# Turning the neighbour sums of a graph layer once, with the repeats made by transfers in SBUF, and one-hots made two sets ahead

## The chip, the cores and the metric

The kernel runs on one core of one Trainium2 chip. The metric is device time in microseconds (us). The engines are called as in the profile: PE is TensorE's matmul (PEld its weight load), DVE is VectorE, ACT is ScalarE, POOL is GpSimd, and SP is SyncE, which here only issues DMAs.

## What is computed

Two graph layers on 6250 nodes with 160 features (64 scalars and 32 vectors of three components) and 100000 edges sorted by target. The first layer, whose last part the change is in, sums messages by node and then takes a tensor product of each node's own features with its sums:

```python
msgs = _merge(m0 + d0, m1 + d1)
agg = jax.ops.segment_sum(msgs, row, num_segments=N)
a0, a1 = _split(agg)                       # 64 scalars, 32 x 3
x0, x1 = _split(node_features)
u0, u1 = _tp(x0, x1, a0, a1, wu000, wu011, wu101, wu110)
ud0, ud1 = _lin(x0, x1, lu0, lu1)
return node_features + _merge(u0 + ud0, u1 + ud1)
# in _tp:
out0 = (einsum('eu,ev,uvw->ew', x0, y0, w000) + INV_SQRT3 * einsum('euk,evk,uvw->ew', x1, y1, w110)) / sqrt(fan0)
out1 = (einsum('eu,evk,uvw->ewk', x0, y1, w011) + einsum('euk,ev,uvw->ewk', x1, y0, w101)) / sqrt(fan1)
```

The second layer gathers, gates and sums again. Here it is enough that it follows.

## The kernel before

Three stages follow each other. `scatter` makes the messages of the edges and writes each to the place in DRAM that its node's bin (25 nodes) has; `update` does the rest of the first layer; `windows` is the second layer. Only `update` is touched.

`update` works by groups of 500 nodes: twelve full ones and one of 250. Features lie on partitions and nodes along the row. For one group:

- `fetch` (L683) loads messages into `urec`, four bins (a set) at a time, 322 KB a bin, by SP's queue. It is called after the set that frees the buffer has been summed; there are three buffers. A group has five sets.
- `sums` (L696) is a generator, with a yield where other work may come between. For each set, `ones` (L702) makes one-hots of the messages' nodes: ACT computes `rl`, then 16 squares (L719) and one Relu (L722) into `uhot`; for group 0 DVE does it instead. PE then sums the set by 16 matmuls (L734), ACT copies the sums into `ag` (L740, L742), and the one-hots of the next set are made.
- After the last set the sums are turned, so that features come to lie on partitions: matmuls of `ag` with `quad` (L755), copied by ACT into `a` (L751). `a` is 128 x 4 x 500. The product needs the 64 scalar sums twice and each 32 vector sums four times over the 128 partitions, so `ag` holds its columns already repeated, and the turning is done four times, once for each part of `a`.
- `Group.first` makes products. A step of kind y, x or v multiplies weights or features on PE into PSUM (L833, L852; two buffers), and DVE multiplies the result with `a` or with `x1k` (L837, L855). POOL adds products of y and v (L840, L860) and prepares parts of v with `a` in `ahead` (L822), from `xb`, which `repeat` (L815) loads. `second` (L868) sums products on PE.
- `back` (L875) finishes a group during the next one: it adds the result to the node's features (L898), normalises (L909 to L920, into `uh`), turns again (L930, `uT` L933), multiplies with the next layer's weights (L940, L941) and stores rows of the table T1 from `utt` (L945, L946; two buffers).

The order on PE, DVE, ACT and POOL is written out by hand: the loop at the end of `update` goes through 32 steps of a group in the pattern y, x, v, x, and in each calls `next` some times on the next group's `sums` and on the last group's `back`:

```python
for _ in range((2, 2, 0, 1)[r % 4] if r >= 3 and g + 1 < len(groups) else 0):
    next(gs[g + 1].sums, end)
for _ in range((1, 2, 0, 1)[r % 4]):
    while backs and next(backs[0], end) is end:
        backs.pop(0)
```

So where a matmul of `sums` falls depends on how many yields stand before it. The order of DMAs on SP's queue is not written out; a scheduler sets it when the kernel is built. SP takes its queue in order, and each DMA there waits for its inputs, for its buffer, and, as the eight semaphores of these DMAs are used in turn, for the DMA that had its semaphore before.

The sums of group 0 have no earlier group to run beside; they are made ahead of the loop.

Of the kernel before, what the change touches and what calls it, by code (L numbers as in the profile page):

```python
# [13 lines left out]
F32 = mybir.dt.float32  # L14
# [9 lines left out]
P = 128  # L24
M0, M1 = 64, 32
V = 3 * M1
F = M0 + V
# [6 lines left out]
BW = 25  # L34
# [22 lines left out]
def gnn_kernel(ctx: ExitStack, tc: tile.TileContext, a: dict, out: bass.AP):  # L57
    nc = tc.nc
# [564 lines left out]
    def update():  # L623
# [3 lines left out]
        with ExitStack() as s:  # L627
            wp = s.enter_context(tc.tile_pool(name="uw", bufs=1))
            pool = s.enter_context(tc.tile_pool(name="u", bufs=1))
            two = s.enter_context(tc.tile_pool(name="u2", bufs=2))  # L630
# [7 lines left out]
            pt = s.enter_context(tc.tile_pool(name="pt", bufs=2, space=PSUM))  # L638
# [33 lines left out]
            quad = wp.tile([P, 4, BW], F32, name="quad")  # L672
# [10 lines left out]
            def fetch(k):  # L683

                if k >= len(quads):
                    return
                g, q = quads[k]
                b0, nq = groups[g][0] // BW + q, min(4, groups[g][1] // BW - q)
                got[g, q] = recs.tile([P, 4, 4, F + 1], F32, name="urec")
                for b in range(nq):  # L690
                    with tc.issue_after(last[-1]) if last else nullcontext():
                        at = nc.sync.value_load(start_i[0:1, b0 + b:b0 + b + 1], min_val=0, max_val=E)
                    last.append(nc.sync.dma_start(got[g, q][:, b], msgs[bass.ds(at, CAP), :]
                                                  .rearrange("(p i) f -> p i f", i=4)).ins)

            def sums(g, a):  # L696

                r0, n = groups[g]
                qs = [(q, min(4, n // BW - q)) for q in range(0, n // BW, 4)]
                hots, ags = [], []  # L700

                def ones(q, nq):  # L702


                    rl = two.tile([P, 4, 4], F32, name="rl")
                    nc.scalar.activation(rl[:, :nq], got[g, q][:, :nq, :, F], AF.Copy, scale=-1.0,
                                         bias=float(r0 + q * BW))
                    hot = two.tile([P, 4, 4, 32], F32, name="uhot")
                    hots.append(hot)
                    if g == 0:  # L710
                        nc.vector.tensor_tensor(hot[:, :nq].rearrange("p b i n -> p i b n"),
                                                node[:, None, :nq].to_broadcast([P, 4, nq, 32]),
                                                rl[:, :nq].rearrange("p b i -> p i b")[:, :, :, None]
                                                .to_broadcast([P, 4, nq, 32]), op=OP.add)
                        nc.vector.tensor_single_scalar(hot[:, :nq], hot[:, :nq], 0.0, op=OP.is_equal)
                        return
                    for b in range(nq):
                        for i in range(4):
                            nc.scalar.activation(hot[:, b, i], node[:, b], AF.Square, bias=rl[:, b, i:i + 1])  # L719
                        if b % 2:  # L720
                            yield
                    nc.scalar.activation(hot[:, :nq], hot[:, :nq], AF.Relu, scale=-1.0, bias=1.0)  # L722
                    yield

                yield from ones(*qs[0])
                yield
                for j, (q, nq) in enumerate(qs):
                    if g == 0 and j + 1 < len(qs):
                        yield from ones(*qs[j + 1])
                    p = pt.tile([P, 4 * P], F32, name="ptr")  # L730
                    rec, hot = got.pop((g, q)), hots.pop(0)
                    for i in range(4):
                        for b in range(nq):
                            nc.tensor.matmul(p[32 * b:32 * b + 32, :F], hot[:, b, i], rec[:, b, i, 0:F],  # L734
                                             start=i == 0, stop=i == 3, tile_position=(0, 32 * b))
                    fetch(quads.index((g, q)) + 3)
                    yield
                    w = 32 * nq
                    ag = pool.tile([P, 4, P], F32, name="ag", bufs=5)
                    nc.scalar.copy(ag[:w, 0].rearrange("p (i f) -> p i f", i=2),  # L740
                                   p[:w, None, 0:M0].to_broadcast([w, 2, M0]))
                    nc.scalar.copy(ag[:w, 1:].rearrange("p k (i f) -> p k i f", i=4),  # L742
                                   p[:w, M0:F].rearrange("p (k f) -> p k f", k=3)[:, :, None]
                                   .to_broadcast([w, 3, 4, M1]))
                    ags.append(ag)
                    if g and j + 1 < len(qs):
                        yield from ones(*qs[j + 1])
                    yield
                for j in range(5):
                    if j:  # L750
                        nc.scalar.copy(a[:, j - 1, :n], p[:, :n])  # L751
                    if j < 4:
                        p = pt.tile([P, 4 * P], F32, name="ptr")
                        for ag, (q, nq) in zip(ags, qs):
                            nc.tensor.matmul(p[:, q * BW:(q + nq) * BW], ag[:32 * nq, j],  # L755
                                             quad[:32 * nq, :nq].rearrange("p b n -> p (b n)"), start=True, stop=True)
                        yield

            def loads(g, n):

# [27 lines left out]
            class Group:  # L788
                def __init__(self, g):
                    self.g = g  # L790
                    self.r0, self.n = groups[g]
                    self.a = two.tile([P, 4, 4 * P], F32, name="a")
                    self.side = loads(g, self.n)
                    self.sums = sums(g, self.a)
                    self.early = {}
                    self.begun = False
# [981 lines left out]
```

## Time and profile before

| | us |
|---|---|
| median of 3 runs (lowest to highest) | 3754.78 (3748.99 to 3765.18) |
| the profiled execution | 3762.7 |
| its span | 3760.6 |
| scatter, in the span | 0 to 1376 |
| sums of group 0 | 1376 to 1411 |
| update of all groups | 1411 to about 2337 |
| windows | about 2337 to 3760 |

The profile shows one execution. A group of its lines stands for all instructions of one line of code on one engine. A wait is written as who waited, on what, for whom, with the total of us, the number and the longest. In a timeline a line has its start, its length, the engine, the line of code, the operation, out<-in and a count, and in brackets the idle time before it and what ended it.

### The profile page before, as it was taken

Reading aid. Unit: us, or ns where it says so; the run is one execution under the profiler, and the core shown is the slowest. Engines: PE = TensorE matmul, PEld = TensorE weight load, DVE = VectorE, ACT = ScalarE, POOL = GpSimd, SP = SyncE. Lnnn points to the kernel's source line nnn. Section 1 sums busy time; section 2 is a strip of 40 time slices with the busy share of each in tenths; the row PEclk is TensorE's granted clock in tenths of the full one; section 3 lists DMA queues with packets and bytes.
Section 4 is the critical chain, followed back from the end, with each engine's and each line's share of the span. In section 5 each row is a group of like instructions: output and inputs, shape, how many; then the busy total and the mean of one; then the engine's idle time right before and its main releaser. Section 6 shows DMA issues by size and latency. Waiting matters only on the chain. (4 is left out here: it accounts for less than half of the span.)

```text
span 3760.6 us, 47934 instructions
## 1 busy us (share of the span) xinstructions
PE 2411.6 (64%) x12112; PEld 1273.7 (34%) x12112; DVE 2218.5 (59%) x4577; ACT 1547.0 (41%) x5126; POOL 2219.3 (59%) x1864
## 2 busy tenths in 40 slices
PE   5555565565544439999999998455655565655655
PEld 3433343343333323333333333132323333332323
DVE  7665555555444427777777775455555556555554
ACT  4554444554444424544453441333434333433433
POOL 4655555555666537777777775655555555555552
PEclk8677767776666659999999999566666666666666
DMA  6655555555444456665565532445444454445442
GB/s 176 172 162 162 151 160 174 153 171 153 135 132 130 135 178 179 181 181 159 173 182 176 165 116 70 130 131 147 133 136 132 135 141 139 132 134 146 134 132 71
DMA packets 346121, 554.56 MB, mean 147 GB/s; under 512 B 63954, under 2 KB 245168, under 8 KB 339947
## 3 DMA queue, kind: packets, MB, share of 16 engines
q1 hardware_dynamic: 229160, 288.49, 27.7%
q0 software_dynamic: 87584, 218.31, 19.9%
q10 hardware_dynamic: 29091, 44.61, 3.6%
q8 instruction: 99, 1.62, 0.2%
q14 instruction: 187, 1.53, 0.1%
HBM read 418.16 MB, written 133.04 MB: 147 GB/s over the span
## 5 line engine op out<-in xcount | busy, mean ns | idle before, releaser
L563 POOL DMA_INDIRECT msgs<-rec,pos_i x782 | 782.5, 1001 | 568.2 <-issue 223.9
L1060 POOL DMA_INDIRECT wgot<-T,src_i x782 | 741.3, 948 | 636.0 <-issue 423.7
L543 PE MATMUL rank<-seen,every 128*128 128x256 f16 x782 | 261.2, 334 | 449.3 <-ACT junk L556 296.5
L556 ACT ACTIVATE junk<-rank,off 128x256 bf16<-128x256 f32 x782 | 373.2, 477 | 403.5 <-remote 284.5
L545 PE MATMUL pmsg<-tw,d 120*128 120x160 f32 x1564 | 463.4, 387 | 79.8 <-issue 68.8
L1079 PE MATMUL wgate<-wrad,wblk 97*128 97x480 f32 x522 | 378.6, 858 | 175.0 <-issue 133.3
L855 DVE TENSOR_TENSOR pr<-y,a 128x1000 f32<-128x1000 f32 (+1 forms) x312 | 352.7, 1153 | 132.7 <-PE y L852 131.9
L840 POOL TENSOR_TENSOR pr<-pr 128x1500 f32<-128x1500 f32 (+1 forms) x104 | 338.1, 3251 | 149.1 <-DVE pr L837 149.1
L1097 DVE TENSOR_TENSOR whot<-lane,wbank 128x192 f32<-128x192 f32 x131 | 45.9, 350 | 619.4 <-ACT wbank L1205 550.1
L1216 PE MATMUL wbank<-wms,whot 128*32 128x160 f32 x1564 | 255.7, 411 | 213.6 <-ACT wo L1220 104.5
L545 PEld LDWEIGHTS pmsg<-tw,d 120*128 120x128 f32 x1564 | 317.0, 251 | 147.4 <-issue 93.4
L1091 ACT ACTIVATE wm<-wgot,wattr 128x160 f32<-128x160 f32 x782 | 311.1, 398 | 34.9 <-DMA wgot<-T,src_i 12.6
L560 DVE CAST pos_i<-pos 128x4 int32<-128x4 f32 x196 | 42.4, 216 | 419.1 <-ACT junk L556 347.5
L1216 PEld LDWEIGHTS wbank<-wms,whot 128*32 128x32 f32 x1564 | 146.4, 144 | 405.9 <-ACT wo L1220 137.5
L1094 ACT ACTIVATE wsg<-wgate 128x480 f32<-128x480 f32 x259 | 137.5, 566 | 352.7 <-remote 187.7
L860 POOL TENSOR_TENSOR ppr<-ppr,pr 128x1000 f32<-128x1000 f32 (+1 forms) x104 | 232.0, 2231 | 79.5 <-DVE pr L855 77.1
L544 PEld LDWEIGHTS <-upto 128*128 128x128 bf16 x782 | 91.6, 117 | 541.5 <-issue 499.3
L544 PE MATMUL rank<-hot,upto 128*128 128x256 bf16 x782 | 262.2, 335 | 0.5 <-DVE hot L528 0.5
L531 DVE TENSOR_TENSOR seen<-seen,hot 128x256 f16<-128x256 f16 x782 | 230.5, 295 | 45.5 <-DVE hot L528 7.6
L528 DVE TENSOR_SCALAR hot<-binb,qb 128x256 bf16<-128x256 bf16 x782 | 242.7, 310 | 0.0
L1079 PEld LDWEIGHTS wgate<-wrad,wblk 97*128 97x128 f32 x522 | 131.2, 285 | 314.2 <-issue 239.6
L1115 DVE TENSOR_TENSOR wm<-wm,wtb 128x384 f32<-128x384 f32 (+1 forms) x393 | 221.8, 564 | 13.5
(215 smaller groups left out, 4430.2 us busy)
## 6 DMA issues: line engine op xcount, KB each, us to landing
urec<-msgs SPq DMA_DIRECT2D x250, 322.0 KB
attb<-in_attr SPq DMA_DIRECT2D x48, 960.0 KB
tw<-T0s SPq DMA_DIRECT2D x391, 75.0 KB
xb<-hT SPq DMA_DIRECT2D x192, 125.0 KB
dstb<-in_dstrow SPq DMA_DIRECT2D x48, 480.0 KB
T0s<-tt ACTq DMA_DIRECT2D x11, 1200.0 KB
msgs<-rec,pos_i POOLq DMA_INDIRECT x782
wgot<-T,src_i POOLq DMA_INDIRECT x782
```

What stands on the lines that cost most here:

```text
L528: nc.vector.tensor_scalar(hot, binb, qb[:, t:t + 1], None, op0=OP.is_equal)
L543: nc.tensor.matmul(rank[:, j % 2], every, before, start=True, stop=False)
L544: nc.tensor.matmul(rank[:, j % 2], upto, hot, start=False, stop=True)
L545: nc.tensor.matmul(prs[-1][:, j % 2, :F], ds[j // WP][:, j % WP], tws[j // WP], start=True, stop=True)
L556: nc.scalar.activation(junk, rank, AF.Relu, bias=off, accum_out=pos[:, j:j + 1])
L563: nc.gpsimd.indirect_dma_start(out=views[(t0 + j) % NV][:, :], out_offset=bass.IndirectOffsetOnAxis(ap=pos_i[:, j:j + 1], axis=0), in_=rec ...
L840: nc.gpsimd.tensor_tensor(prs[0], prs[0], prs[1], op=OP.add)
L855: nc.vector.tensor_tensor(pr[:, :, :n], y[:, :, :n], a[:, j, None, :n].to_broadcast([P, 2, n]), op=OP.mult)
L1060: nc.gpsimd.indirect_dma_start(out=got[u][:, i], out_offset=None, in_=T1[:, :], in_offset=bass.IndirectOffsetOnAxis(ap=src_i[:, t0 + i:t0 ...
L1079: nc.tensor.matmul(p[:, :n], blocks[u // CH][:, u % CH], rad[:, lo * F:lo * F + n], start=True, stop=True)
L1091: nc.scalar.activation(m[:, b, j:j + F], g[:, i, oS1:oS1 + F], AF.Copy, scale=attr(u)[:, i, 0:1])
L1216: nc.tensor.matmul(state["acc"][j:j + WN], hot[:, i], ms[:, i], start=t0 + i == w * WT, stop=t0 + i == end, tile_position=(0, j))
```

## The change

`ag` becomes a plain copy of a set's 160 sums. The turning is done twice: columns 0 to 127 (the 64 scalars and the first two vector components) and columns 128 to 159. ACT copies each of the four parts once into `a`, at the partitions where it comes out of the matmul, and DMAs within `a` fill the other partitions: one of 64 rows and nine of 32 rows of 2000 bytes a group. They go by SP's queue; for group 0 six of the ten go by ACT's. The one-hots of two sets are made before the first set is summed (except in group 0), and those of set j + 2 after set j; `rl` and `uhot` get a third buffer. The number of yields in `sums` changes with it.

```diff
@@ -702,10 +702,10 @@
                 def ones(q, nq):
 
 
-                    rl = two.tile([P, 4, 4], F32, name="rl")
+                    rl = two.tile([P, 4, 4], F32, name="rl", bufs=3)
                     nc.scalar.activation(rl[:, :nq], got[g, q][:, :nq, :, F], AF.Copy, scale=-1.0,
                                          bias=float(r0 + q * BW))
-                    hot = two.tile([P, 4, 4, 32], F32, name="uhot")
+                    hot = two.tile([P, 4, 4, 32], F32, name="uhot", bufs=3)
                     hots.append(hot)
                     if g == 0:
                         nc.vector.tensor_tensor(hot[:, :nq].rearrange("p b i n -> p i b n"),
@@ -722,7 +722,8 @@
                     nc.scalar.activation(hot[:, :nq], hot[:, :nq], AF.Relu, scale=-1.0, bias=1.0)
                     yield
 
-                yield from ones(*qs[0])
+                for q, nq in qs[:1 if g == 0 else 2]:
+                    yield from ones(q, nq)
                 yield
                 for j, (q, nq) in enumerate(qs):
                     if g == 0 and j + 1 < len(qs):
@@ -736,25 +737,26 @@
                     fetch(quads.index((g, q)) + 3)
                     yield
                     w = 32 * nq
-                    ag = pool.tile([P, 4, P], F32, name="ag", bufs=5)
-                    nc.scalar.copy(ag[:w, 0].rearrange("p (i f) -> p i f", i=2),
-                                   p[:w, None, 0:M0].to_broadcast([w, 2, M0]))
-                    nc.scalar.copy(ag[:w, 1:].rearrange("p k (i f) -> p k i f", i=4),
-                                   p[:w, M0:F].rearrange("p (k f) -> p k f", k=3)[:, :, None]
-                                   .to_broadcast([w, 3, 4, M1]))
+                    ag = pool.tile([P, F], F32, name="ag", bufs=5)
+                    nc.scalar.copy(ag[:w], p[:w, 0:F])
                     ags.append(ag)
-                    if g and j + 1 < len(qs):
-                        yield from ones(*qs[j + 1])
+                    if g and j + 2 < len(qs):
+                        yield from ones(*qs[j + 2])
                     yield
-                for j in range(5):
-                    if j:
-                        nc.scalar.copy(a[:, j - 1, :n], p[:, :n])
-                    if j < 4:
-                        p = pt.tile([P, 4 * P], F32, name="ptr")
-                        for ag, (q, nq) in zip(ags, qs):
-                            nc.tensor.matmul(p[:, q * BW:(q + nq) * BW], ag[:32 * nq, j],
-                                             quad[:32 * nq, :nq].rearrange("p b n -> p (b n)"), start=True, stop=True)
-                        yield
+
+
+                for lo, hi in ((0, P), (P, F)):
+                    p = pt.tile([P, 4 * P], F32, name="ptr")
+                    for ag, (q, nq) in zip(ags, qs):
+                        nc.tensor.matmul(p[:hi - lo, q * BW:(q + nq) * BW], ag[:32 * nq, lo:hi],
+                                         quad[:32 * nq, :nq].rearrange("p b n -> p (b n)"), start=True, stop=True)
+                    yield
+                    for j, at, w in ((0, 0, M0), (1, M0, M1), (2, M0 + M1, M1)) if lo == 0 else ((3, 0, M1),):
+                        nc.scalar.copy(a[at:at + w, j, :n], p[at:at + w, :n])
+                        for to in range(0, P, w):
+                            if to != at:
+                                (nc.scalar if g == 0 and to // w % 2 else nc.sync).dma_start(
+                                    a[to:to + w, j, :n], a[at:at + w, j, :n])
 
             def loads(g, n):
 
```

## The prediction

> **What bounds the kernel now.** I read the 40 slices first, then the busy time by stage, then who waits for whom inside the stage that the change touches, then one group of that stage in order of time.
>
> ```profile
> PE   5555565565544439999999998455655565655655
> ...
> PEclk8677767776666659999999999566666666666666
> ```
> ```profile
> 1376.00:1411.00 35.00, 18.10 (x200) 14.09 (x200) 5.60 (x10) 5.66 (x18) 0.00 (x0) 0.53 0.90 269
> 1411.00:2256.00 845.00, 783.36 (x5125) 290.80 (x5123) 650.38 (x606) 379.82 (x1392) 628.86 (x232) 0.99 0.57 168
> ```
>
> The first fence has the slices: those with 9s on PE are the update (1411 to 2330 us), the only stage in the diff. The second has two stages (length, then busy us of PE, PEld, DVE, ACT, POOL, then PE's clock, DMA share, GB/s). In the update PE is busy 783 of 845 us, at a clock of 0.99; DVE, POOL and ACT have 23%, 26% and 55% to spare. So work taken off PE is worth its time, unless another wait grows. The 35 us before it, when group 0 is summed, are DMA-bound (share 0.90), with PE half idle. A group of 500 nodes takes 73.2 us and has 32 steps, in fours y, x, v, x; I number them 0 to 31.
>
> ```profile
> L755 PEld LDWEIGHTS ptr<-quad,ag x504: 183/192/338, 1404.6 to 2255.8; 128*128 128x128 f32 x168
> L755 PE MATMUL ptr<-quad,ag x504: 272/275/537, 1404.6 to 2255.9; 128*128 128x100 f32 x168
> ```
> ```profile
> PE ptr L734 <- ACT uhot L722: 17.6, 10, 1.9
> PE y L852 <- DVE pr L837: 12.8, 20, 1.1
> PE ptr L734 <- DVE uxo L898: 9.7, 9, 1.1
> PE ptr L940 <- ACT utt L945: 6.1, 10, 0.6
> PE ptr L894 <- ACT ag L742: 3.1, 10, 0.3
> PE ptr L755 <- ACT utt L945: 2.4, 2, 1.6
> ```
>
> The first two lines are the turning, by the tile ag; the others are PE's own waits over ten steady groups (us in total, times, longest). The wait for one-hots, L734 on L722, is the largest: 1.76 us a group.
>
> ```profile
> 1907.25 2.73 PE L755 MATMUL ptr<-quad,ag 128*128 128x100 f32 x20
> 1909.82 0.59 PE L852 MATMUL y<-x,pick 96*128 96x500 bf16 x2
> 1910.33 1.06 PE L868 MATMUL out<-pr,w_f 128*64 128x500 f32 x4
> 1911.32 2.48 PE L755 MATMUL ptr<-quad,ag 128*128 128x100 f32 x20
> 1913.63 0.59 PE L852 MATMUL y<-v,pickv 96*128 96x500 bf16 x2
> ```
> ```profile
> 1899.66 4.15 SPq L693 DMA_DIRECT2D urec<-msgs  x4
> 1903.91 0.85 SPq L946 DMA_DIRECT2D T<-utt  x2
> 1904.85 0.97 SPq L815 DMA_DIRECT2D xb<-hT  x2
> 1908.59 0.29 SPq L946 DMA_DIRECT2D T<-utt  x1
> 1908.93 1.71 SPq L815 DMA_DIRECT2D xb<-hT  x4
> ```
> ```profile
> 1908.09 0.48 ACT L945 COPY utt<-ptr 116x384 f32<-116x384 f32 x1 [6.27 <-DMA T<-utt]
> ```
>
> This is the tail of one group in order of time, on PE, SP's queue and ACT (start, us, instruction). Twenty turning matmuls hold PE 2.31 us (1911.32 to 1913.63), 0.1155 us each. In the middle ACT stands 6.27 us on a store of T1 that SP could only issue after the four loads of urec; PE's second turning needs the PSUM buffer which that ACT copy empties.
>
> **The change part by part.** *Turning.* The 504 instructions become 252. Group 0 loses 20; groups 1 to 11 lose 20 each and the half group 6 of 12: 11 x 20 + 12 = 232 in the PE-bound stage, 232 x 0.1155 = 26.8 us saved. The second turning has 32 stationary columns; I give it the same pitch, since 100 columns stream either way. If it were as short as L734's with 32 columns (0.04 us an instruction), up to 9 us more would go.
>
> *ACT.* The two copies into ag (266 and 484 ns) become one of 160 columns; between those rows that is about 0.29 us, so 0.46 us less, five times a group. The copies into a stay four; fewer partitions do not shorten them (L751, 576 ns for 500 columns). ACT has room, so both count as nothing while that holds.
>
> *Ten transfers a group within a* (one of 128 KB, nine of 64 KB). No such row exists. Issue: the nearest is xb on the same queue, four in 1.71 us, so ten take 4.3 us. Landing: in group 0 POOL starts on xb 3.3 us after the last of its loads is issued (1414.3 to 1417.65); urec of 322 KB, four issued from 1389.27, is used at 1396.17. A rule of the Trainium skill speaks against this part: DMA: Bandwidth & Descriptors, section "Anatomy of one DMA", gives (for the GpSimd path) about 2.0 us fixed plus bytes at 436 GB/s, and its "Bandwidth" section calls transfers under 64 KB dominated by descriptors. By it, taken one after another, ten cost 10 x 2.15 = 21.5 us; by the rows above they overlap, 4.3 + 3.3 = 7.6 us. I take the rows. From the start of the second turning: ACT's last copy ends 2 us later, SP issues from 0.6 to 5, the last lands at about 8. The next group's first y, where PE (L833), DVE (L837) and POOL (L822) all need a, comes after 12.3 us (1908.62 to 1923.25 in the trace of this group, less the 2.3 removed). So the repeats are hidden with some 4 us to spare; behind them on SP stands x0 of a later group, which waits for PE's last y anyway. Their 0.7 MB add a twentieth to a group's traffic (173 GB/s over 73 us).
>
> *One-hots two sets ahead.* In the built order, the sums' matmuls (L734) move from steps 5, 9, 13, 17, 21 to 8, 12, 16, 20, 21. The 1.76 us wait goes. What is late next? SP's order moves too: two loads of xb now precede the fetch of the fourth set, and they wait until POOL has read the old xb (L822, 1793.26 to 1795.57 in the group that starts at 1774.41). The fetch starts near 1796.4, needs 3.8 us to issue and 2 to 3 to land: 1802.4 to 1803.3. ACT's one-hots of that set now stand ahead of the normalisation of the group before. From there ACT needs 3.7 + 1.1 + 1.9 (uh) + 0.6 + 0.3 + 3.7 (the fifth set) + 1.0 (uT) = 12.3 us, so uT is ready at 1814.7 to 1815.6. PE reaches the matmul on uT (L940) at about 1814.5; from there to the fifth set's matmul it has 6.8 us, now with the fourth set's in between: 1821.5 to 1822.4, against 1822.36 in the trace. So the wait that goes comes back almost whole as waits for uh, uT and DVE: gain 0 to 0.8 us a group. I take 0.3, 3 us in all; bounds are the whole 17.6 us and, by one more such ACT delay, -10.
>
> *The T1 store.* Fourth and fifth sets are now fetched back to back: 8 x 322 KB in 8 us, issued at 339 GB/s, while DMA here reaches 268 to 287 GB/s. The backlog grows from about 0.5 to 1.2 us; the T1 store behind it lands 0.7 us later, then ACT's utt copy, then PE's second turning, which now has no slack (2.4 us of waits in ten groups): -0.7 x 10 = -7 us, bounds 0 and -15.
>
> *Group 0.* Nothing hides its repeats. SP is issuing urec until 1411.36, so its four transfers go out at 1411.4 to 1413.1 and land about 1416; six go by ACT's queue, some 0.4 us each between the copies. DVE started at 1412.40: -3.5 us, bounds -1 and -6.
>
> The third buffers of rl and uhot are paid for by the smaller ag and cost nothing. Scatter and windows stages keep their instructions.
>
> Sum: 26.8 + 3 - 7 - 3.5 = 19 us off the profiled execution's 3762.7 (span 3760.6 plus 2.1 around it). That execution lies 0.2% above the median shown, 3754.78; the same share gives 3736. A measurement of this kernel can tell about 0.5%, 18.8 us, from no change, so the likeliest case ends almost on that bound.
>
> **The rivals.** *A: one-hots ahead pay in full.* If urec lands early and uh is not late, all 17.6 us go and the T1 store costs 2: 26.8 + 17.6 - 2 - 3.5 = 39 us, 3716. For it: the wait was named in every group. Against it: the SP order and the ACT chain above. *B: the waits eat it.* DVE paces steps 4 to 12 (PE loses the filler of one sums matmul there, DVE has uxo and statistics to add) and the bad bounds of one-hots and T1 store hold: 26.8 - 10 - 15 - 3.5 = -2 us, 3757, no change. For it: PE already waits on L837 and L898. *C, slower: the repeats land late.* Its place is the first y of each group. It takes over from a last landing 12.3 us after the second turning starts, and each us beyond costs 11; from 14 us on the gain is gone. Taken one by one at 2.15 us, the last lands at 22.1, 9.8 late: 108 - 19 = 89 us slower, 3844; with a third of that lateness, 3772. For it: the SP queue is in order and waits for ACT there. Against it: four xb loads issue in 1.7 us without waiting for each other. That the change fails to take work off PE can be excluded: the built order has half the turnings.
>
> **How the numbers follow.** Likeliest case 0.42 (3728 to 3746, half of it past 0.5%), A 0.26, B 0.19 (a little of it slower), C 0.13. Faster by over 0.5%: 0.21 + 0.26 + a little of B's good end = 0.49. Slower: C and B's bad end, 0.14. Within: 0.37. The range goes from A with shorter second turnings, 3706, to the mild end of C, 3774.
>
> **What would show it.** L755 (now L751) has 252 instructions; PE busy in 1411 to 2256 falls by about 27 us. PE's wait of L734 for uhot is gone; in its place PE waits for uT before the first L940 and for utt before the second turning, 0.5 to 1 us each. DVE's first multiply of a group never waits for a transfer within a, except in group 0, where it starts 3 to 4 us later. A group takes 71.5 to 72 us. Wrong: a group under 70.5 us (A); DVE or PE waiting on a's transfers at every group's first step (C); PE busy down by 27 us but groups still at 73 us (B).

## The result and the profile after

The changed kernel takes 3767.43 us (median), the kernel before 3756.39 us beside it: ratio 1.0026, 95% interval 1.0016 to 1.0036, some 10 us slower, inside the 0.5% that was set as the bound. The prediction had it 19 us faster. A second measurement (e8 below) gave 1.0011 (0.9996 to 1.0027). So the change costs a few microseconds, where 19 were forecast as won.

The kernels below were measured in several rounds, not all on one chip: the kernel before took 3756, 3078, 3726, 3762 and 3077 us in them. Each ratio is to the kernel before in the same round. What differs between the rounds lies outside the update; the loop over groups inside it, from the first to the last product of x with the self weights (L804 before), does not move with it, so I compare *loops* across runs: 872.2 us before (869.9 in e11) and 870.8 after (861.0 in e8, and 869.3 in e3, whose loop has the same code, in the round at 3078). One execution of a loop is good to some 5 us either way.

First the slices of the page of the changed kernel, then its stage of 845 us that answers to 1411:2256 (length, busy us of PE, PEld, DVE, ACT, POOL, PE's clock, DMA share, GB/s), and the turning by its tile:

```profile
PE   5555555656444438889899898356655555555655
...
PEclk8666677767666658999999999566666666666666
```
```profile
1424.50:2269.50 845.00, 762.88 (x4890) 266.50 (x4891) 649.68 (x606) 353.66 (x1314) 627.44 (x232) 0.97 0.61 176
```
```profile
L751 PE MATMUL ptr<-quad,ag x252: 204/275/536, 1410.5 to 2266.6; 128*128 128x100 f32 x62, 128*32 128x100 f32 x62, 64*128 64x50 f32 x1, 64*32 64x50 f32 x1
```

The turning has half its instructions and PE is busy 20 us less in the stage. But the digits of PE in the update went from 9 to 8 and 9, and its clock from 0.99 to 0.97: the work went away and time did not. Who PE waits for in ten steady groups (us, times, longest):

```profile
PE y L854 <- DVE pr L839: 16.6, 30, 1.1
PE ptr L751 <- ACT utt L947: 11.0, 9, 3.5
PE y L835 <- DVE pr L857: 10.8, 18, 0.7
PE ptr L896 <- DVE uxo L900: 8.7, 5, 4.3
PE ptr L942 <- ACT uT L935: 6.5, 10, 1.6
PE ptr L942 <- ACT utt L947: 6.1, 10, 0.6
PE y L854 <- DVE pr L857: 5.1, 10, 0.5
```

The wait for one-hots is gone, as forecast, and most others have grown or are new: 69 us in all against 54 before. The line to follow is `uxo`. DVE adds the finished group to uxo, and waits for its load; first the changed kernel, then the kernel before, from the waits of DVE in the same ten groups:

```profile
DVE uxo L900 <- DMA uxo<-xs: 19.2, 9, 5.5
```
```profile
DVE uxo L898 <- DMA uxo<-xs: 4.1, 2, 3.9
```

The tail of the group that starts at 1799.18, on SP's queue and on ACT, answers to the tail shown before:

```profile
1840.12 8.29 SPq L693 DMA_DIRECT2D urec<-msgs  x8
1848.52 1.66 SPq L948 DMA_DIRECT2D T<-utt  x2
...
1853.79 0.29 SPq L948 DMA_DIRECT2D T<-utt  x1
1854.25 6.98 SPq L758 DMA_DIRECT2D a<-a  x10
```
```profile
1853.29 0.48 ACT L947 COPY utt<-ptr 116x384 f32<-116x384 f32 x1 [7.67 <-DMA T<-utt]
```

Eight fetches stand back to back, and the T1 store behind them keeps ACT 7.67 us in place of 6.27. Behind the store come the ten transfers, 6.98 us on SP's queue.

Group 0, on SP and on DVE, and DVE's first product before:

```profile
1394.89 26.24 SPq L693 DMA_DIRECT2D urec<-msgs  x20
1421.24 2.53 SPq L758 DMA_DIRECT2D a<-a  x4
```
```profile
1426.24 1.72 DVE L839 TENSOR_TENSOR pr<-y,a 128x1500 f32<-128x1500 f32 x1 [18.18 <-DMA a<-a]
```
```profile
1412.40 1.72 DVE L837 TENSOR_TENSOR pr<-y,a 128x1500 f32<-128x1500 f32 x1 [10.31 <-PE y L833]
```

DVE's first product starts 13.84 us later than before. Of these, 6.3 us are another end of scatter in that execution: ACT's first `rl` is at 1384.06 against 1377.74, and in e9 and e10, where nothing of group 0 is by transfers, the loop's start (1423.4 and 1426.9 against 1416.8 before) wanders as far. From that `rl` to DVE's first product it is 42.18 us after and 34.66 before: 7.5 us are the change's.

### The profile page after: what moved, and what is told of

Same layout as the page of the kernel before. It is cut to its first block, busy times and chain, and to the rows that moved or that the text cites. A ratio compares the mean times of both kernels' runs of the same rounds, so it can differ in the third digit from the quotient of the medians.

```text
span 3766.4 us, 47528 instructions
## 1 busy us (share of the span) xinstructions
PE 2388.1 (63%) x11860; PEld 1249.2 (33%) x11860; DVE 2213.0 (59%) x4577; ACT 1521.9 (40%) x5063; POOL 2214.9 (59%) x1864
## 5 line engine op out<-in xcount | busy, mean ns | idle before, releaser
L545 PE MATMUL pmsg<-tw,d 120*128 120x160 f32 x1564 | 471.6, 393 | 69.5 <-issue 58.4
L1081 PE MATMUL wgate<-wrad,wblk 97*128 97x480 f32 x522 | 368.9, 839 | 161.3 <-issue 122.2
L839 DVE TENSOR_TENSOR pr<-y,a 128x1500 f32<-128x1500 f32 (+1 forms) x104 | 172.2, 1656 | 101.4 <-PE y L835 75.5
```

The costliest lines, as they stand in the source:

```text
L545: nc.tensor.matmul(prs[-1][:, j % 2, :F], ds[j // WP][:, j % WP], tws[j // WP], start=True, stop=True)
L1081: nc.tensor.matmul(p[:, :n], blocks[u // CH][:, u % CH], rad[:, lo * F:lo * F + n], start=True, stop=True)
```

## The experiments

Three questions: what does the halved turning bring by itself, what do its transfers cost and by what, and what do the one-hots cost? Theory 1 after reading the trace was that the transfers cost only in group 0 and that the one-hots' new order on SP makes uxo late; theory 2 that the transfers make it late.

**e1: turning and transfers alone.** The kernel before, with these lines of the change and nothing of the one-hots:

```diff
+                    ag = pool.tile([P, F], F32, name="ag", bufs=5)
+                    nc.scalar.copy(ag[:w], p[:w, 0:F])
...
+                for lo, hi in ((0, P), (P, F)):
```

> The turning and its ten transfers of the changed kernel; the one-hots as before (one set ahead, two buffers). Theory 1 (the one-hots two ahead cost more than they save, by the order on SP: uxo and T1 stores later; the transfers cost only in group 0): PE loses its 27 us, no new waits in the steady groups, group 0 costs about 7 us: 20 us under the kernel before, ratio 0.995 (0.993 to 0.996). DVE's wait for uxo stays near 4 us in ten groups. Theory 2 (the transfers themselves load SP's queue and the DMA engines in each group and make the other loads late): no faster than before, 0.998 to 1.003, with the uxo wait near 19 us here too.

Measured: ratio 0.9993 (0.9982 to 1.0003), loop 859.8 us, DVE's wait for uxo 32.4 us in ten groups. Theory 1 fails: uxo is late without any change of the one-hots. SP's queue at a group's end and the next one's begin shows why; behind it are the loads of x1 and uxo of the kernel before, in the group of the prediction:

```profile
1419.85 6.25 SPq L755 DMA_DIRECT2D a<-a  x10
1426.14 1.07 SPq L814 DMA_DIRECT2D xb<-hT  x2
1427.31 0.48 SPq L761 DMA_DIRECT2D x<-hT  x1
1428.15 1.25 SPq L766 DMA_DIRECT2D x1k<-hT  x3
1438.57 0.31 SPq L763 DMA_DIRECT2D x<-hT  x1
...
1442.73 1.80 SPq L814 DMA_DIRECT2D xb<-hT  x4
1444.58 0.86 SPq L307 DMA_DIRECT2D uxo<-xs  x2
```
```profile
1781.68 0.32 SPq L764 DMA_DIRECT2D x<-hT  x1
...
1784.59 0.85 SPq L307 DMA_DIRECT2D uxo<-xs  x2
```

At 1429.4 the queue stops for 9 us: L763 loads x1, whose one buffer is free only when PE has multiplied the old x1 (L804 there). Behind that stop are eleven loads that stand ahead of uxo, among them four of xb; uxo goes out 6.0 us after x1. Before, five loads stood between the two and uxo followed 2.9 us after x1. With ten transfers ahead of the stop, six loads that stood there before have come behind it: four of xb, one of x1k and one of x3. In the changed kernel three of xb stand there (issued from 1876.00, after the tail above).

The lateness costs twice. PE's clock in stretches around one such wait (same columns as above), and two of its instructions:

```profile
1370.90:1374.30 3.40, 1.74 (x9) 0.56 (x7) 0.88 (x2) 3.11 (x13) 1.65 (x1) 1.00 0.80 216
1374.30:1374.90 0.60, 0.02 (x1) 0.00 (x0) 0.60 (x2) 0.00 (x0) 0.00 (x0) 0.52 0.91 176
1374.90:1381.10 6.20, 6.20 (x17) 1.74 (x19) 5.39 (x6) 0.00 (x0) 5.25 (x3) 0.50 0.67 207
```
```profile
1373.80 0.43 PE L893 MATMUL ptr<-both,u 128*128 128x64 f32 x2 [1.66 <-DVE uxo L897]
...
1374.90 1.20 PE L832 MATMUL y<-x,w_f 64*128 64x500 f32 x1 [0.58 <-DVE pr L854]
```

PE waits 1.66 us and works 0.5; then, as a second wait of 0.58 us only begins, the granted clock is half, and it stays so for over 6 us: the same matmul that took 0.68 us takes 1.20. The Trainium skill ("TensorE: Matmul & The Clock Gate", "HAM oscillation — how this bites in real kernels") has the rule that gaps of PE beyond about 3.4 us bring the half clock; here it came after one of 1.66 us. Such a wait does not always bring it: PE waits up to 1.9 us for one-hots in every group of the kernel before, at a clock of 0.99. What decides it is not shown here.

**e6: the turning without transfers**, as e1, with a set to zero once and no DMA within it, so that the repeats are left out:

```diff
-                    self.a = two.tile([P, 4, 4 * P], F32, name="a")
+                    self.a = abuf[g % 2]
...
-                        for to in range(0, P, w):
-                            if to != at:
-                                (nc.scalar if g == 0 and to // w % 2 else nc.sync).dma_start(
-                                    a[to:to + w, j, :n], a[at:at + w, j, :n])
```

> As e1, but without any transfer within a (the repeats are left out of the computation; a is set to zero once). What the halved turning is worth by itself. If the prediction's first term is right: PE busy 26 us lower, no new wait, loop 845 (843 to 848), ratio 0.991. If the wait for one-hots or DVE's pace takes back what PE saves: loop 852 or more, ratio 0.994 or more.

Measured: ratio 0.9902 (0.9877 to 0.9927), loop 835.8 us: 36 us less than before, 24 less than e1. Its ten steady groups, then those of e1 (columns as above), and all of PE's waits over 3 us in e6:

```profile
1460.00:2159.50 699.50, 653.37 (x4282) 227.99 (x4281) 562.48 (x531) 316.48 (x1171) 543.13 (x201) 1.00 0.63 182
1212.80:1941.50 728.70, 667.59 (x4281) 230.40 (x4280) 562.48 (x531) 316.40 (x1171) 543.52 (x202) 0.98 0.64 183
```
```profile
PE ptr L738 <- ACT uhot L726: 14.0, 10, 1.4
PE y L851 <- DVE pr L836: 12.5, 20, 1.1
PE ptr L738 <- DVE uxo L897: 10.1, 10, 1.2
PE ptr L939 <- ACT utt L944: 6.1, 10, 0.6
```

The halved turning is worth more than forecast: PE is busy 653.4 us against 682.8 before, no new wait came up in these groups, and ACT, whose copies are shorter, took 3.6 us from the wait for one-hots and the whole 3.1 and 2.4 of the waits for ag and, before the turning, utt. Against e1, the transfers cost 15 us of PE idle (its wait for uxo ahead of L893 is 17.3 us there and 2.1 here) and 14 us of PE busy (667.6 against 653.4) in ten groups. That is 29 us, where the loops differ by 24: e6's group 0 has one wait of PE for POOL of 5.0 us, which is at most 1.7 us in every other run and says nothing of the turning. So where a run is compared with e6, the ten groups are the better measure.

**e5: the transfers on ACT's queue.** As e1, but:

```diff
-                                (nc.scalar if g == 0 and to // w % 2 else nc.sync).dma_start(
+                                nc.scalar.dma_start(
```

and group 0 by PE as in e3. SP's order is then the one without transfers.

> As e1 (turning and transfers of the changed kernel, one-hots as before), but all transfers of the steady groups are issued by ACT's queue, right behind the copies that they repeat, and group 0's repeats are made by PE as in e3. SP's queue then has the order that it has without any transfer. Theory Q (the steady transfers cost by their place on SP's queue: four xb loads and the uxo load fall behind the wait of x1 for the group's first sums): loop 845 to 850 us from the first to the last product of x with the self weights (872 before, 860 in e1), DVE's wait for uxo at most 5 us in ten groups, ratio 0.992 (0.991 to 0.994). Theory B (they cost by the bytes that they move or by landing late): loop 856 to 862, uxo wait over 15 us or a new wait for a, ratio 0.996 to 0.998.

Measured: ratio 0.992 (0.9894 to 0.9947), loop 839.6 us, wait for uxo 4.6 us. The same bytes moved at the same time cost 5 us in ten groups here (704.8 against 699.5) and 29 on SP's queue. So they cost by their place, not by their traffic. ACT has room there: it waited 141.7 us in ten groups for the group's last sums in e6 and still waits 86.6 here.

**e12: a second buffer for x1.** As e1, with the transfers on SP's queue, group 0's too:

```diff
-                x1 = pool.tile([V, 4 * P], F32, name="x1")
+                x1 = two.tile([V, 4 * P], F32, name="x1")
```

> e1 with one word changed: x1 has two buffers. The order on SP's queue stays that of e1 but for the place of x1's second load; that load no longer stops the queue until PE has read the old x1 (1438.57 in the group that starts at 1436.48 in e1), so the 13 loads behind it go out earlier; the four xb loads can go when POOL has read the old xb (1436.1), uxo about 6 us earlier than in e1 (1438.8 in place of 1445.4), landing before DVE asks for it (1445.5). Theory Q (the steady transfers cost because they pushed these loads behind that wait): DVE's wait for uxo falls from 32 to at most 6 us in ten groups, PE's clock is 0.99 to 1.00 again in place of 0.98, loop 836 to 843 (860 in e1), and with group 0's transfers still in, ratio 0.993 to 0.995. Rival (the transfers themselves are slow or fill the queue): loop over 852, ratio 0.998 or more.

Measured: ratio 0.9953 (0.9935 to 0.9971), loop 840.2 us, PE's clock 1.00 in the ten groups.

```profile
1418.14 0.58 SPq L763 DMA_DIRECT2D x<-hT  x1
...
1425.21 8.27 SPq L814 DMA_DIRECT2D xb<-hT  x4
1433.52 0.86 SPq L307 DMA_DIRECT2D uxo<-xs  x2
```

x1 goes out at once; the queue now stops inside the four xb loads (8.27 us, 1.80 in e1). DVE still waits 19.5 us for uxo, not the 6 that I expected, but no longer at a bad place: PE waits for it 6.2 us in place of 17.3, and the slow stretches are gone but for one in the first of the ten groups. The ten groups take 710.5 us: one word gives back 18 of the 29 us (20 of 24 by the loops), so the stop at x1 was the place where most of them were lost. Of the other 11, 4 are PE's wait for uxo (2.1 in e6); the rest is not taken apart here.

**e7: uxo asked for early.** The changed kernel, with the load of uxo at step 20 of its own group:

```diff
+                    if r == 20:
+                        gs[g].features()
```

> The changed kernel with one edit: the load of a group's features into uxo is asked for at step 20 of that group, not after its last sums, so that it stands ahead of the transfers within a on SP's queue. Theory Q: DVE's wait for uxo (19 us in ten groups) goes, the loop falls from 871 to 856 to 860 us, ratio to before 0.998 to 1.000. Rival: the load was only the first of several that the transfers make late (x1k, xb), and the time is lost at the next of them: loop over 865, ratio 1.001 or more.

Measured: ratio 1.0086 (1.0061 to 1.0111), loop 884.2 us: the rival's outcome, though the time is lost at the T1 store, which it did not name. DVE never waits for uxo any more. But uxo and four xb loads now go out ahead of the first T1 store, and with them a set's fetches, which wait for PE. In the group looked at, the first utt is copied by 1725.9 and its store issued at 1732.78; ACT then waits 6.87 us for that buffer, and PE 4.20 us for ACT. PE's largest wait, and the clock around that one (the wait ends at 1737.48):

```profile
PE ptr L946 <- ACT utt L951: 40.8, 10, 4.8
```
```profile
1730.00:1735.00 5.00, 3.28 (x40) 1.64 (x40) 1.20 (x1) 0.08 (x1) 3.36 (x1) 1.00 0.93 260
1735.00:1740.00 5.00, 2.52 (x6) 1.22 (x6) 0.00 (x0) 0.70 (x2) 0.00 (x0) 0.63 0.98 300
1740.00:1745.00 5.00, 5.00 (x15) 0.95 (x14) 2.40 (x2) 0.48 (x1) 3.37 (x2) 0.69 0.65 218
```

A gap of 4.2 us, and the ten microseconds from its middle on read 0.63 and 0.69: here the skill's rule (section as above) and the trace agree. Mending one load of an in-order queue moved the stop to another.

**e3: group 0 by PE.** The changed kernel; in group 0 each part is turned once for every place where it is needed:

```diff
+                if g == 0:
...
+                            for to in range(0, P, w):
+                                nc.tensor.matmul(p[to:to + w, q * BW:(q + nq) * BW], ag[:32 * nq, at:at + w],
...
+                                                 stop=True, tile_position=(0, to))
```

> The changed kernel, but group 0's repeats made by PE (70 matmuls of 64 or 32 columns in place of 20 and the ten transfers); all other groups unchanged. Theory 1: the transfers of group 0 cost 7 to 8 us of the 13.8 by which its first product came later, the rest being another end of scatter in that execution: 7 us under the changed kernel, so ratio to the kernel before 1.0008 (1.000 to 1.0015). Rival: all 13.8 us are theirs: 0.999. Rival: all of it was scatter's end: 1.0026, as the changed kernel.

Measured: ratio 0.9998 (0.9989 to 1.0007), loop 869.3.

```profile
1133.99 1.72 DVE L849 TENSOR_TENSOR pr<-y,a 128x1500 f32<-128x1500 f32 x1 [8.85 <-PE y L845]
```

From ACT's first rl (1100.76) to this product it is 33.2 us, 9 less than in the changed kernel: group 0's transfers cost 7.5 us against before and 9 against the better way. Fifty more matmuls on PE cost nothing that shows there; the stage had a DMA share of 0.90 and a PE half idle before.

**e2: one-hots two ahead alone**, on the turning of before (tiles shortened from 512 to 500 columns to make room):

```diff
-                yield from ones(*qs[0])
+                for q, nq in qs[:1 if g == 0 else 2]:
+                    yield from ones(q, nq)
```

> The one-hots two sets ahead of the changed kernel; the turning with repeats on PE, no transfers, as before. So that the third one-hots fit, the rows of four kinds of tiles (a, x1k and DVE's products) are 500 long in place of 512. Theory 1: the wait for one-hots (17.6 us) goes, and waits for uxo (plus 15), T1 stores (plus 9) and uT, uh and DVE (plus 10) come: 10 to 20 us slower than before, ratio 1.003 to 1.005. Theory 2: without the transfers the loads are on time and the 17.6 us are won: 0.995 to 0.997.

Measured: ratio 1.0068 (1.0052 to 1.0085), loop 900.1: slower by 21 us, the loop by 28. DVE's wait for uxo is 3.2 us: that part of theory 1 is wrong here too, and it cost more than either theory had. PE's waits for DVE's products are 27.9 us in ten groups (13.4 before), for uT 11.1 (none before), for utt ahead of the turning 9.8 (2.4). DVE is busy 563.3 us there and 562.8 before, so the shorter tiles did not slow it.

**e4: the changed kernel without transfers.** The edit of e6, on the changed kernel.

> The changed kernel without any transfer within a: a has two fixed buffers that are set to zero once, and each part is written only at the partitions where it comes out of the turning, so the repeats are left out of the computation. Theory 1: transfers cost only in group 0; as with its repeats by PE or 1 to 3 us less, ratio to before 1.000 to 1.001; DVE's wait for uxo stays near 19 us. Theory 2: the steady transfers cost too: 0.995 to 0.997, and the uxo wait falls to about 4.

Measured: ratio 0.9941 (0.9927 to 0.9955), loop 852.1, uxo wait 5.0. Against e3 the steady transfers cost 17 us of loop here; against e6, which differs by the one-hots alone, these cost 16, and 21 in ten groups (720.1 against 699.5).

**e9 and e10: the one-hots on kernels with the transfers out of the way.** e9 is e5 with the one-hots of the change. e10 makes the same one-hots as early on ACT, but leaves PE's instructions in the order of e5, the half group at the end excepted:

```diff
+                yield from ones(*qs[0])
+                if g:
+                    for _ in ones(*qs[1]):
+                        pass
...
+                    elif g and j + 1 < len(qs):
+                        for _ in range(qs[j + 1][1] // 2 + 1):
+                            yield
```

> As e5 (transfers by ACT's queue, group 0's repeats by PE), plus the one-hots two sets ahead as in the changed kernel. If these cost by themselves, as the pair e4 and e6 says (852 against 836 us of loop): 16 us more than e5, loop 853 to 858, ratio to before 0.996 to 0.997; uxo wait under 6 us; PE waits for uT, utt and uxo's steps in place of the wait for one-hots. If they cost only where SP's queue is late: loop 836 to 841, ratio 0.991 to 0.992.

> As e9, but the second set's one-hots are made at once behind the first's, and yields are put where the last set's one-hots were, so that PE's order is that of e5 to the instruction; only ACT makes the one-hots a set earlier. If the place of the sums' matmuls is what costs in e9 (4 to 12 steps later, two sets back to back, the T1 store behind eight fetches): the wait for one-hots (14 us in ten groups) goes and nothing comes, loop 826 to 832, ratio 0.988 to 0.990. If it is ACT's order (the normalisation and uT behind a set of one-hots): PE waits for uh and uT, loop 840 to 855.

Measured: e9 0.9975 (0.9964 to 0.9986), loop 863.9; e10 0.9907 (0.9888 to 0.9925), loop 842.6. So the one-hots of the change cost 24 us of loop against e5 (839.6), and 21 of these come with the place of the sums' matmuls. First PE's waits of e9, then of e10, then one of e5:

```profile
PE y L864 <- DVE pr L849: 16.8, 30, 1.1
PE ptr L761 <- ACT utt L957: 8.7, 8, 2.6
PE ptr L952 <- ACT uT L945: 7.9, 10, 1.3
PE y L845 <- DVE pr L867: 6.9, 11, 0.7
```
```profile
PE y L869 <- DVE pr L854: 14.9, 20, 1.4
PE ptr L737 <- issue: 8.2, 9, 0.9
PE ptr L947 <- ACT uT L950: 6.4, 10, 0.6
PE ptr L911 <- ACT ag L743: 3.7, 8, 0.5
```
```profile
PE ptr L734 <- DVE uxo L907: 9.1, 9, 1.1
```

In e9 PE waits for DVE in the steps that a matmul of sums used to fill, and for utt behind the eight fetches. In e10 both are back to near the size of e5 (14.5 us for DVE; utt ahead of the turning 1.6 in e5, 2.7 in e10). The wait for one-hots, 14 us in e5, is gone in e10 too, and yet the loop is no shorter: in its place PE waits 6.4 us for uT, whose copy ACT now makes behind a set of one-hots, 3.7 for ag, and 2 more than in e5 for uxo ahead of L911 and utt together, and it is busy 659.4 us against 656.6. The 8.2 us at L737, for which the profile has no releaser, are no part of it: they lie 16 to 18 us after a group's first product with the self weights, where e5 has its 9.1 us for uxo, shown last. My 826 to 832 is missed; the second case of the expectation, ACT's order, came true. The wait for one-hots could be moved but not won.

**e8 and e11: the two kernels again.**

> The changed kernel once more, beside the others. Loop 869 to 873 us, ratio to before 1.002 to 1.004.

> The kernel before once more, for the scatter of the loop between executions of one program (the changed kernel's was 871 and 861): 868 to 874 us, ratio 1.000.

Measured: e8 1.0011 (0.9996 to 1.0027), loop 861.0, both below what I expected; e11 0.9989 (0.9979 to 0.9999), loop 869.9. The program of before, against itself, reads 0.1% off; a difference of that size is none.

## Why the prediction was wrong

In loops: 871 before (mean of two); the turning takes it to 836 (e6), the transfers on SP's queue to 860 (e1), the one-hots to 867 (mean of the changed kernel's 870.8, 861.0 and e3's 869.3). With 7.5 us in group 0 that makes 4 us slower, where the two ratios say 4 and 10. By the steps of the prediction:

- **Turning**, 26.8 us: right in kind, too small. Alone it took 35 us of loop (33 to 38 in ten groups, 699.5 against 737.3 and 732.0); PE busy fell by 29.4 us in ten groups against before, 26.3 against e11 (679.7), where the forecast's price gives 23.1, and some 8 us are waits that shrank with ACT's shorter work, which the prediction costed at nothing.
- **Ten transfers**, "hidden with some 4 us to spare": the step that failed. They did land in time: in steady groups of the changed kernel no engine waited for a. The issue took 0.6 to 0.7 us each, waits for ACT's copies included, not 0.43, and the skill's serial 21.5 us never showed: in the tail above DVE multiplies with a at 1867.27, 13.0 us after the first of the ten was issued. That choice between row and rule was right in outcome. What was wrong is the sentence after it, that behind them on SP "stands x0 of a later group, which waits for PE's last y anyway". x0 did stand there, but with it xb, x1k, x1 and uxo. In e1 the scheduler moved six of these loads past the stop at x1, and uxo came 3 us later behind it; in the changed kernel three of xb stand between the two. PE lost 29 us in ten groups by it (e1 against e6), half in waits and half in busy time at a lower clock; in the order of the changed kernel the loss is 17 us of loop (e3 against e4). e5 and e12 take 24 and 18 of the 29 back in two ways.
- **One-hots two ahead**, +3: the sign was wrong. The prediction saw the wait come back "as waits for uh, uT and DVE" and let it come back less than whole; e4 against e6 and e9 against e5 say 16 (21 by the ten groups) and 24 us more than whole, T1 store included, against the forecast's -4. What it put into rival B alone ("PE loses the filler of one sums matmul") was the largest term: PE's waits for DVE's products are 28.8 us in e9 and 14.8 in e5, while those for uT and utt grew by 8 and 7.
- **The T1 store**, -7: right. PE's wait of the turning for utt is 8.6 to 11.0 us in e4, e9, e8 and the changed kernel, 2.4 before. Its 339 GB/s is a slip, though: eight times 322 KB in 8 us are 330, and the measured 8.29 us make 318.
- **Group 0**, -3.5: -7.5, outside the bound of -6. SP's 20 fetches took 26.24 us in place of 22.09, so that its own four transfers were issued 3.5 us later (counted from the first rl) than the sum had them; that is most of what was missing. One fetch waited 3.9 us for a transfer of ACT's queue, through the semaphores that both queues use in turn: in the other runs with transfers in group 0 (e1, e7, e8, e12) the 20 fetches take 25.7 to 26.4 us, in all without them 21.7 to 22.2.
- **PE's clock** was in no term. It cost about half of what the transfers cost in e1: 14 us of PE's busy time, with the same instructions.

The likeliest case and rival A did not happen; the time lies in the range, by rival B's outcome (PE's busy time down, ten groups in 738.2 us, 737.3 before), though a good half of the mechanism was SP's queue, which B did not name. C was wrong: nothing waited for the repeats in steady groups.

The two best kernels here, e10 and e5, are 0.9% and 0.8% faster than before, and their intervals overlap; both use the half turning, ACT's queue for its repeats and PE for group 0's. e10's early one-hots add nothing to e5 that these runs show.

## What to carry to other kernels

Before a DMA is called hidden, write down what stands behind it on its in-order queue, and where that queue next stops for a buffer: what is pushed past the stop comes late, and delays what already stood behind it. Put new transfers on the queue of an engine that is idle just then, or take the stop away with a second buffer. And a matmul between two vector steps may be what hides them: a wait taken from one place of a hand-written order is won only if the place it moves to has slack.

## What the runs showed of the hardware

One gap of PE of 1.66 us was followed by half a clock over more than 6 us (e1), while waits up to 1.9 us in every group left the kernel before at 0.99; around a gap of 4.2 us the clock read 0.63 and 0.69 over 10 us (e7). In e1 eight stretches at half clock, of 3 to 7 us, lie in ten groups, and PE's busy time is 14 us longer than in e6 with the same instructions: a part of a wait's cost shows as busy time.

Transfers of 64 KB within SBUF took 0.6 us each to issue, on SP's queue as on ACT's (three in 1.80 us in e10), and hardly slowed the rest so far as the ten groups show (5 us of 700, e5 against e6).
